# Layer-1 stacks with a gap behind each pair, and two heads of a pair in one 32-column tile

## Chip, cores and metric

The kernel runs on one core of a Trainium2 chip. The metric is the device time of one execution in microseconds (us). The core has a matrix engine (TensorE: PE for the matmuls, PEld for the weight loads), VectorE (DVE), ScalarE (ACT), GpSimd (POOL) and a queue engine (SyncE, SP) that issues nearly all DMAs. Data live in SBUF (128 partitions), matmul results in PSUM (eight banks of 128 x 512 f32), and intermediate tensors in DRAM.

## Reference

Two decoder layers on x (32 batch rows, 128 positions, 128 channels), each a post-norm chain of three blocks: layer 0 has a recurrent mix, a block of two attentions with an FC part, and an expert layer; layer 1 has a rotary self-attention, a cross-attention with silu in place of softmax, and an expert layer with capacities. The edit touches the first two blocks of layer 1:

```python
q = split_heads(x @ Wq + bq)          # 16 heads of 8
k = split_heads(x @ Wk + bk)
v = split_heads(x @ Wv + bv)
q, k = _rope(q), _rope(k)
scores = einsum('bhqd,bhkd->bhqk', q, k) / sqrt(8)
probs = softmax(scores)
out = einsum('bhqk,bhkd->bhqd', probs, v) ...  @ Wo + bo
# cross-attention: scores as above from x and ctx, masked, then
attn = silu(scores); out = einsum('bhqk,bhkd->bhqd', attn, v) ... @ Wo.T
```

## The kernel before

The 32 batch rows are worked on in eight groups of four (G = 4, GT = 512 tokens). Each block of a layer is a stage that yields, for each group, eight units with lags; the list `items` holds every step at its place and `pipeline` emits the steps in that order. The framework's scheduler then plans the order on each engine's queue from estimated durations and gives out the buffers of each pool (`w8`: seven slabs of 2,064 f32 columns; `PT`: two PSUM banks; `PV`: one, called the bank). Stages overlap: the self-attention (stage 5) starts under the expert layer of layer 0 (stage 4), and the cross-attention (stage 6) starts under the end of stage 5.

**Stacks.** Scores of layer 1 are computed from three bf16 parts of the f32 queries and keys. Heads have 8 channels, so the parts of one head are stacked into 48 rows. `spill` (L829 to L832) writes the parts of a group to a DRAM tensor `d_st` whose rows are [2 pars][8 pairs][query and key][512 tokens], and `stack` (L843) reads back, for one half of the heads and one parity, 48 or 50 rows of four pairs each: 8 KB in one piece per row. `scratch` (L816) fills the rows from 48 on from a constant. A group has four such reads: `take` issues two (one per parity) for each of the two halves.

**One self-attention step** j (0 to 7 in a group) is one half of the heads, h = j // 4, and one batch row, b = j % 4. `smax` computes the scores without the maximum (48 rows) and takes row maxima on DVE (L1000). `mrow`, `mwrite` and `mread` turn the maxima into two more rows of the stack by way of DRAM (`d_m`, L1013 and L1019). `probs` computes the scores again with these rows (50 rows) and exponentiates two banks on ACT (L1027). `values9` multiplies by V: V is kept per batch row as a tile of 16 x 9 columns (8 channels and a one for the sum of each head), and eight matmuls take 24 columns each, so that each head fills a block of 32 PSUM rows, four heads beside each other and two parities one after the other in columns. A copy on ACT (L875) brings 256 columns of the bank to `ob`. After both halves of a batch row, `norm` turns `ob` with four transposes (L1038), takes the reciprocal of the sums (L1041) and multiplies (L1044); `oproj` turns the result (L1056) and multiplies by Wo (L1062).

**V tiles.** `pad9` and `more9` cut V tiles out of `w8` slabs and preset them: POOL writes the ones and zeros (L858). `v9proj` adds the bias into them (L925); there are 20 for eight groups, used in turn. In the cross-attention, `valuesx` already lets two heads add into one 32-column block (L1194 is its copy of 128 columns); its V tiles (`vx`, L906) are slabs of `w8` too, and so are the expert weights of layer 1 (`cap_w13`, L1252).

`block` emits a list of matmuls that stay together (L169). All score and value matmuls of layer 1 have this line.

Of the kernel before, what the change touches and what calls it, by code (L numbers as in the profile page):

```python
# [9 lines left out]
F32 = mybir.dt.float32  # L10
FR = mybir.dt.float32r
BF = mybir.dt.bfloat16
U8 = mybir.dt.uint8
I32 = mybir.dt.int32
AF = mybir.ActivationFunctionType
ALU = mybir.AluOpType
# [3 lines left out]

G = 4
GT = G * 128

# [3 lines left out]
W8 = 7  # L29
VX = 10  # L30
V9 = 5
WV = 24
VT = 15 * 9 + WV

BUFS = dict(big=5, v=8, qk=3, e=6, pt=4, xs=4, cs=5, xb=2, msk=2, res=2, x=4)
TAG = dict(y="x", rres="res", wstage="xs", sx="xs", sc="cs", mask0="msk", v="v", qk="qk", e="e", p="pt",
           o="big", wo="big", sot="x", sxb="xb", sres="res", ctx="res", fx="xs", fxb="v", fh="big", fres="res", x1="x", fres2="res", lt="res",
# [35 lines left out]
class Net:  # L73
    def __init__(self, ctx, tc, a, ngroups):
# [15 lines left out]
        nc.gpsimd.tensor_copy(self.identb, self.ident)  # L90
        self.mhalf = self.cst.tile([128, G], F32, name="mhalf")
        nc.gpsimd.memset(self.mhalf, -0.5)
# [14 lines left out]
    def tok(self, tag):  # L107
        return self.t(tag, [G, 128])

# [93 lines left out]
    def half_turns(self, pts, es):  # L203

        calls = []
        for h in range(2):
            for b in range(G):
                for z in range(2):
                    r = slice(z * 64, z * 64 + 64)
                    calls.append((pts[z][:, (h * G + b) * 64:(h * G + b) * 64 + 64], es[h][r, b * 128:(b + 1) * 128],  # L210
                                  self.ident[r, r], None))
# [8 lines left out]
    def putx(self, g, x, final=False, queue=None):  # L220
        if final:
            d = self.a["out"][g * G:(g + 1) * G].rearrange("b s d -> s b d")
        else:
# [586 lines left out]
    def scratch(self, k):  # L810

        if self.dst is None:
            self.dst = []
            for i in range(3):
                d = self.dp.tile([64, 2, 8, 2, GT], BF, name=f"d_st{i}")
                self.nc.sync.dma_start(out=d[48:64], in_=self.a["pad_bf"])  # L816
                self.dst.append(d)
        return self.dst[k % 3]

# [4 lines left out]
    def spill(self, k, p):  # L824

        dma = self.nc.sync.dma_start
        d = self.scratch(k)
        rows = lambda lo, n: d[lo * 8:(lo + n) * 8].rearrange("(a d) r q z t -> (d r q) a z t", d=8)
        dma(out=rows(0, 3), in_=p)  # L829
        for z in range(2):  # L830
            dma(out=rows(3, 2)[:, :, z, :], in_=p[:, z:z + 2, z, :])
        dma(out=rows(5, 1)[:, 0], in_=p.rearrange("p a z t -> p (a z) t")[:, 0:6:5, :])  # L832
        return d

    def stack(self, d, h, n, slab=False):

        if slab:
            s = self.wp.tile([128, 4128], BF, name="w8", tag="w8", bufs=W8)
            s = s[:, 0:8 * GT].rearrange("p (q z t) -> p q z t", q=4, z=2)
        else:  # L840
            s = self.t("stack", [4, 2, GT], BF)
        for par in range(2):
            self.nc.sync.dma_start(out=s[par * 64:par * 64 + n], in_=d[0:n, par, h * 4:h * 4 + 4])  # L843
        return s

    def pad9(self):

        self.v9 = []
        t = self.w8()
        self.more9(t[:, 768:2064])  # L850
        return t[:, 0:768]

    def more9(self, t):
        for k in range(min(t.shape[1] // VT, V9 * G - len(self.v9))):
            c = t[:, k * VT:k * VT + VT]
            v = c[:, 0:144].rearrange("p (h c) -> p h c", c=9)
            self.nc.gpsimd.memset(v[:, :, 8:9], 1.0)
            self.nc.gpsimd.memset(c[:, 144:VT], 0.0)  # L858
            self.v9.append((v, c))

    def values9(self, j, v, ps, ob, last, scale=1.0):

        nc = self.nc
        pq, at = j // 4, j % 2
        o = self.bank()
        calls = []
        for par in range(2):
            c = (at * 2 + par) * 128
            for k in range(4):
                h = 2 * (pq * 4 + k) + par  # L870
                calls.append((o[k * 32:k * 32 + WV, c:c + 128], v[:, h * 9:h * 9 + WV], ps[par][:, k * 128:(k + 1) * 128],
                              dict(start=True, stop=True, tile_position=(0, k * 32))))
        self.block(calls, last)
        ob = ob or self.t("ob")
        nc.scalar.activation(ob[:, pq * 256:pq * 256 + 256], o[:, at * 256:at * 256 + 256], AF.Copy, scale=scale)  # L875
        return ob

    def bank(self):
# [36 lines left out]
    def v9proj(self, g, b, kh, kl, wh, wl, bv):  # L915

        vp = self.pst("v9")
        t = slice(b * 128, (b + 1) * 128)
        self.mm3(vp[:, 0:128], kh[:, t], kl[:, t], wh, wl)
        k = (g + 1) % V9 * G + b  # L920
        if k >= len(self.v9):
            self.more9(self.w8())
        v, c = self.v9[k]
        h8 = lambda t: t.rearrange("p (h d) -> p h d", d=8)
        self.nc.vector.tensor_tensor(v[:, :, 0:8], h8(vp[:, 0:128]), h8(bv), ALU.add)  # L925
        return c

    def att_w(self):
# [10 lines left out]
    def att_units(self, g, getw, done):  # L939
        nc, sm = self.nc, self.sm  # L940
        w = Later(getw)
        st = {}
# [91 lines left out]
        def norm(b):  # L1034
            ob = st.pop(("ob", b))
            tp = self.pst("norm")
            for s in range(4):
                nc.tensor.transpose(tp[:, s * 128:(s + 1) * 128], ob[:, s * 128:(s + 1) * 128], self.ident)  # L1038
            tv = tp.rearrange("p (h c) -> p h c", c=32)
            r = sm.tile([128, 16], F32, name="ar")  # L1040
            nc.vector.reciprocal(r, tv[:, :, 8])  # L1041
            if b == 0:
                st["ok"] = self.t("ok", [G, 16, 8])
            nc.vector.tensor_tensor(st["ok"][:, b], tv[:, :, 0:8], r.unsqueeze(2).to_broadcast([128, 16, 8]), ALU.mult)  # L1044

        def again():
            st["x"] = self.getx(g)
# [5 lines left out]
        def oproj():  # L1053
            tp = self.pst("oT")
            for b in range(G):
                nc.tensor.transpose(tp[:, b * 128:(b + 1) * 128], st["ok"][:, b].rearrange("p h d -> p (h d)"),  # L1056
                                    self.ident)
            oT = self.t("oT")
            nc.scalar.copy(oT, tp)
            o = self.pst("aout").rearrange("p (b d) -> p b d", d=128)  # L1060
            for b in range(G):
                nc.tensor.matmul(out=o[:, b, :], lhsT=oT[:, b * 128:(b + 1) * 128], rhs=w["wo"],  # L1062
                                 start=True, stop=True)
            res = st.pop("res")
            nc.vector.tensor_tensor(res, o, res, ALU.add)
            st["ln"] = self.ln(res, 1e-5, act=True)

        units = []
        for j in range(8):
            h = j // 4  # L1070
# [17 lines left out]
            if j == 7:  # L1088
                o = L6["oproj"]
# [475 lines left out]
def prep(i):  # L1565
    c = np.ascontiguousarray
    f = np.float32
    pairs = lambda w: c(w.reshape(8, 128, 128).transpose(1, 0, 2).reshape(128, 1024))
    d = {
        "xtok": c(i["x"].transpose(1, 0, 2)),  # L1570
        "xT": c(i["x"].transpose(2, 0, 1).reshape(128, 4096)),
        "ctxT": c(i["ctx_1024"].transpose(2, 0, 1).reshape(128, 4096)),
        "mask0": c(i["mask_BxS2_bk0"].reshape(4096)),
        "rwkv_w": c(np.concatenate([i["L0_attn_" + n].T for n in ("Wk", "Wv", "Wr", "Wo")], axis=1)),
        "rwkv_v": c(np.stack([i["L0_attn_" + n] for n in
                              ("mix_k", "mix_v", "mix_r", "spatial_decay", "spatial_first")], axis=1)),
    }
# [23 lines left out]
    b = [i["L1_attn_bq"], i["L1_attn_bk"]]  # L1601
    d["a1_b"] = c(np.stack([b[0][order], b[0][partner], b[1][order], b[1][partner]], axis=1))
    d["a1_bv"] = c(i["L1_attn_bv"])
    d["a1_bo"] = c(i["L1_attn_bo"])
    heads = np.array([2 * (pq * 4 + k) + par for pq in range(2) for par in range(2) for k in range(4)])
    rows = (heads[:, None] * 8 + np.arange(8)).reshape(128)
    d["a1_wo"] = c(i["L1_attn_Wo"][rows])
    inv = (np.float32(1.0) / np.power(np.float32(10000.0), np.arange(0, 8, 2, dtype=f) / np.float32(8))).astype(f)
    ang = np.arange(128, dtype=f)[None, :] * inv[order % 4][:, None]
    d["a1_cos"] = c(np.cos(ang).astype(f))  # L1610
# [8 lines left out]
    heads = np.array([8 * pq + 2 * k + par for k in range(4) for pq in range(2) for par in range(2)])  # L1619
# [28 lines left out]
```

## Time and profile before

| | |
|---|---|
| Median of 3 runs | 1808.09 us (1808.03 to 1809.1) |
| Profiled execution: time, span | 1817.27 us, 1815.5 us |
| Granted TensorE clock, mean | 0.961 |
| PE, PEld, DVE, ACT, POOL busy | 90%, 72%, 76%, 67%, 54% |
| DMA | 163.43 MB, mean 90 GB/s |
| Expert layer of layer 0 (L760), last step | 1217 us |
| Self-attention's exponentials (L1027) | 1217 to 1411 us |
| Cross-attention's copies (L1194) | 1390 to 1568 us |

All times of stages count from the span's start. A row of an instruction group names line, engine and operation, what is written from what, the shape and the number of instructions; then the busy time in us and the mean of one in ns; then the idle time of the engine before them, and what ended it. Durations of matmuls overlap, so their sum is more than PE's time. The chain of waits is followed back from the end of the span, at each step to what released it. Tiles have the names of the pools: `v` or `ob` are one pool, `e` are the exponentials, `big` the stacks, `qk` the parts, `S`, `mm`, `PT`, `PV` are PSUM.

### The profile page before, as it was taken

The numbers are of one execution on the slowest core, as the hardware profiler recorded it, in microseconds if no ns is written. First come the engines' busy times: TensorE is split into PE (matmuls) and PEld (weight loads), VectorE is DVE, ScalarE is ACT, GpSimd is POOL, SyncE is SP. The second block draws the span as 40 slices with busy tenths as digits, with TensorE's granted clock in tenths as the row PEclk, the third lists the DMA queues.
The fourth block names the chain that finished last, engine by engine and source line by source line (L and its number), as shares of the span: only waits on it lengthen the run. The fifth ranks groups of instructions, "written<-read, shape, count | busy, mean of one in ns | idle before, by whom it ended". The sixth has DMA issues, their size and how long they took to land.

```text
span 1815.5 us, 45617 instructions
## 1 busy us (share of the span) xinstructions
PE 1628.6 (90%) x15858; PEld 1311.8 (72%) x15858; DVE 1380.2 (76%) x5303; ACT 1214.1 (67%) x3889; POOL 982.6 (54%) x1324
## 2 busy tenths in 40 slices
PE   4898898899999999998899999998877887989898
PEld 2676676777777777776688888876655554778898
DVE  7879888887777777775676667778864775788896
ACT  3786777878888888887744554336666666656654
POOL 4657676777665555564534444345533443446455
PEclk7899999999999999999999999999989998899999
DMA  6100110111110000000123443336667987223222
GB/s 172 36 26 23 41 44 24 33 48 56 49 39 9 27 25 26 27 25 14 58 79 124 167 154 109 108 124 196 182 184 173 246 231 204 93 71 105 82 94 70
DMA packets 86214, 163.43 MB, mean 90 GB/s; under 512 B 12968, under 2 KB 34352, under 8 KB 80368
## 3 DMA queue, kind: packets, MB, share of 16 engines
q1 hardware_dynamic: 83248, 146.89, 27.5%
q0 software_dynamic: 1584, 11.54, 1.5%
q8 instruction: 125, 2.05, 0.5%
q10 hardware_dynamic: 1152, 2.10, 0.3%
q14 instruction: 105, 0.86, 0.2%
HBM read 106.75 MB, written 55.31 MB: 89 GB/s over the span
## 4 chain that ended last, share of the span: by engine, by line
PE 41%; DVE 20%; ACT 15%; POOL 11%; issue 6%; DMA 6%; SPq 1%; POOLq 0%; ACTq 0%; DVEq 0%
ACT e L483 8%; PE mm L157 5%; PE S L771 5%; PE PV L169 4%; PE mm L158 4%; PE mm L159 4%; DVE e L478 4%; PE S L169 3%; POOL x L255 3%; PE mm L541 3%; PE PT L1395 3%; POOL e L487 2%; DMA x<-x 2%; DVE x L263 2%; PE S L620 1%
## 5 line engine op out<-in xcount | busy, mean ns | idle before, releaser
L483 ACT ACTIVATE e<-e,nm 128x128 f32<-128x128 f32 x1024 | 398.8, 394 | 111.8 <-POOL nm L480 111.8
L487 POOL TENSOR_TENSOR e<-e,ri 128x512 f32<-128x512 f32 x256 | 268.4, 1054 | 175.2 <-DVE ri L485 146.2
L478 DVE CUSTOM_DVE_ANT_0 e<-S,msk 128x128 f32<-128x128 f32 x1024 | 227.9, 284 | 12.0 <-PE PT L168 9.1
L483 ACT ACTIVATION_READ_ACCUMULATOR e<-e,nm 128x1 f32 x1024 | 196.2, 192 | 0.0
L169 PEld LDWEIGHTS S<-qk 64*128 64x128 f32 x2048 | 128.3, 190 | 78.0 <-issue 40.6
L169 PE MATMUL S<-qk 64*128 64x128 f32 x2048 | 151.3, 287 | 30.2 <-DVE pt L501 16.3
L169 PE MATMUL PV<-pt,v 128*64 128x128 f32 x2048 | 141.9, 281 | 10.8 <-DVE big L523 10.6
L157 PE MATMUL mm<-xs,w 128*128 128x512 f32 x296 | 130.9, 446 | 16.5 <-ACT xs L150 5.0
L276 POOL TENSOR_SCALAR rsqv<-bmv 128x4 f32<-128x4 f32 (+1 forms) x73 | 22.5, 308 | 215.3 <-DVE bmv L243 179.9
L771 PEld LDWEIGHTS S<-w,v 128*128 128x128 f32 x1024 | 129.1, 191 | 10.2 <-ACT v L760 1.9
L760 ACT ACTIVATE v<-mm,col_moe_b 128x512 f32<-128x512 f32 x128 | 85.6, 686 | 75.4 <-PE mm L159 74.8
L771 PE MATMUL S<-w,v 128*128 128x128 f32 x1024 | 133.9, 276 | 1.7 <-ACT v L760 1.7
L485 DVE RECIPROCAL ri<-su 128x4 f32<-128x4 f32 x256 | 43.6, 172 | 120.7 <-ACT e L483 90.7
L169 PEld LDWEIGHTS PV<-pt,v 128*64 128x64 f32 x2048 | 110.9, 138 | 21.6 <-issue 6.7
L158 PE MATMUL mm<-xs,w 128*128 128x512 f32 x296 | 119.8, 405 | 1.6 <-DVE xs L151 1.4
L159 PE MATMUL mm<-xs,w 128*128 128x512 f32 x296 | 119.1, 402 | 0.0
L169 PE MATMUL PV<-e,w 128*32 128x128 f32 (+1 forms) x2048 | 90.3, 299 | 26.3 <-ACT e L1027 13.9
L501 DVE COPY pt<-PT 128x256 f32<-128x256 f32 x256 | 97.3, 415 | 8.4 <-ACT pt L501 7.6
L523 DVE TENSOR_TENSOR big<-PV,big 128x512 fp32r<-128x512 f32 x128 | 87.3, 682 | 19.5 <-ACT big L522 19.0
L1000 DVE TENSOR_REDUCE amx<-mm 128x4 f32<-128x512 f32 x128 | 82.1, 684 | 24.3 <-PE mm L169 24.2
L501 ACT COPY pt<-PT 128x256 f32<-128x256 f32 x256 | 81.8, 373 | 25.2 <-PE PT L168 25.0
L541 PE MATMUL mm<-big 128*128 128x512 f32 x384 | 96.9, 398 | 0.0
(326 smaller groups left out, 4803.7 us busy)
## 6 DMA issues: line engine op xcount, KB each, us to landing
x<-x SPq DMA_DIRECT2D x151, 256.0 KB
pt<-d_w SPq DMA_DIRECT2D x64, 256.0 KB
big<-d_st SPq DMA_DIRECT2D x32, 400.0 KB
d_st<-qk SPq DMA_DIRECT2D x48, 256.0 KB
d_st<-qk SPq DMA_DIRECT2D x16, 768.0 KB
big<-d_st SPq DMA_DIRECT2D x32, 384.0 KB
d_w<-big POOLq DMA_DIRECT2D x11, 1024.0 KB, 6.4
w<-d_w SPq DMA_DIRECT2D x7, 1024.0 KB
```

Of the source, the lines that this page charges most:

```text
L157: mm(out=out, lhsT=wh, rhs=xh, start=True, stop=False)
L158: mm(out=out, lhsT=wh, rhs=xl, start=False, stop=False)
L159: mm(out=out, lhsT=wl, rhs=xh, start=False, stop=True)
L169: return self.nc.tensor.matmul(out=out, lhsT=lhsT, rhs=rhs, **more)
L478: self.seen = nc.vector.tensor_tensor_reduce(e[:, t], s[h][:, t], msk[:, t], 1.0, NEG, ALU.add, ALU.max, mx[:, b:b + 1])
L483: nc.scalar.activation(e[:, t], e[:, t], AF.Exp, bias=nm[:, b:b + 1], scale=0.125, accum_out=su[:, b:b + 1])
L487: i = nc.gpsimd.tensor_tensor(e3, e3, ri.unsqueeze(2).to_broadcast([128, G, 128]), ALU.mult)
L501: last = (nc.vector.tensor_copy if h else nc.scalar.copy)(d, s_)
L523: nc.vector.tensor_tensor(lo, o, hi.bitcast(F32), ALU.subtract)
L541: nc.tensor.matmul(out=out, lhsT=a_, rhs=b_, start=n == 0, stop=n == 3 * PER - 1)
L760: nc.scalar.activation(h, hp, AF.Gelu, bias=w["b1"][:, k:k + 1])
L771: nc.tensor.matmul(out=o[:, b, :], lhsT=hs[i][:, b * 128:(b + 1) * 128], rhs=w["w2"][:, k * 128:k * 128 + 128], start=i == 0, stop=i == 1)
```

## The change

In DRAM, a row of a stack holds for each pair 1,024 elements and now 8 unused ones (16 bytes), so that the four pairs that one read takes are no longer adjacent; all writes and reads of `d_st`, in stage 5 and 6, follow. In the self-attention a V tile is now 8 x 27 columns: per pair, the even head's 9, nine zeros, the odd head's 9. The matmul of a head takes 18 columns (its own 9 and the zeros), and the two heads of a pair add into the same 18 rows of a block. The copy takes 128 columns in place of 256, `norm` has two transposes in place of four, and Wo is no longer reordered.

```diff
+GAP = 8
-WV = 24
-VT = 15 * 9 + WV
+VT = 8 * 27
...
-                d = self.dp.tile([64, 2, 8, 2, GT], BF, name=f"d_st{i}")
-                self.nc.sync.dma_start(out=d[48:64], in_=self.a["pad_bf"])
+                d = self.dp.tile([64, 2, 8, 2 * GT + GAP], BF, name=f"d_st{i}")
+                self.nc.sync.dma_start(out=d[48:64, :, :, 0:2 * GT], in_=self.a["pad_bf"].rearrange("p r q z t -> p r q (z t)"))
...
-        rows = lambda lo, n: d[lo * 8:(lo + n) * 8].rearrange("(a d) r q z t -> (d r q) a z t", d=8)
-        dma(out=rows(0, 3), in_=p)
+        rows = lambda lo, n: d[lo * 8:(lo + n) * 8].rearrange("(a d) r q x -> (d r q) a x", d=8)
+        dma(out=rows(0, 3)[:, :, 0:2 * GT], in_=p.rearrange("p a z t -> p a (z t)"))
         for z in range(2):
-            dma(out=rows(3, 2)[:, :, z, :], in_=p[:, z:z + 2, z, :])
-        dma(out=rows(5, 1)[:, 0], in_=p.rearrange("p a z t -> p (a z) t")[:, 0:6:5, :])
+            dma(out=rows(3, 2)[:, :, z * GT:(z + 1) * GT], in_=p[:, z:z + 2, z, :])
+        dma(out=rows(5, 1)[:, 0, 0:2 * GT].rearrange("p (z t) -> p z t", z=2), in_=p.rearrange("p a z t -> p (a z) t")[:, 0:6:5, :])
...
-            self.nc.sync.dma_start(out=s[par * 64:par * 64 + n], in_=d[0:n, par, h * 4:h * 4 + 4])
+            self.nc.sync.dma_start(out=s[par * 64:par * 64 + n].rearrange("p q z t -> p q (z t)"),
+                                   in_=d[0:n, par, h * 4:h * 4 + 4, 0:2 * GT])
...
-            v = c[:, 0:144].rearrange("p (h c) -> p h c", c=9)
-            self.nc.gpsimd.memset(v[:, :, 8:9], 1.0)
-            self.nc.gpsimd.memset(c[:, 144:VT], 0.0)
+            v = c.rearrange("p (q r c) -> p q r c", r=3, c=9)
+            self.nc.gpsimd.memset(v[:, :, 1, :], 0.0)
+            v = v[:, :, 0:3:2, :]
+            self.nc.gpsimd.memset(v[:, :, :, 8:9], 1.0)
...
-        pq, at = j // 4, j % 2
-        o = self.bank()
+        pq = j // 4
+        o = self.bank()[:, j % 2 * 128:j % 2 * 128 + 128]
...
-            c = (at * 2 + par) * 128
             for k in range(4):
-                h = 2 * (pq * 4 + k) + par
-                calls.append((o[k * 32:k * 32 + WV, c:c + 128], v[:, h * 9:h * 9 + WV], ps[par][:, k * 128:(k + 1) * 128],
-                              dict(start=True, stop=True, tile_position=(0, k * 32))))
+                c = (pq * 4 + k) * 27 + par * 9
+                calls.append((o[k * 32:k * 32 + 18, :], v[:, c:c + 18], ps[par][:, k * 128:(k + 1) * 128],
+                              dict(start=par == 0, stop=par == 1, tile_position=(0, k * 32))))
...
-        nc.scalar.activation(ob[:, pq * 256:pq * 256 + 256], o[:, at * 256:at * 256 + 256], AF.Copy, scale=scale)
+        nc.scalar.copy(ob[:, pq * 128:pq * 128 + 128], o)
...
-            for s in range(4):
+            for s in range(2):
                 nc.tensor.transpose(tp[:, s * 128:(s + 1) * 128], ob[:, s * 128:(s + 1) * 128], self.ident)
-            tv = tp.rearrange("p (h c) -> p h c", c=32)
-            r = sm.tile([128, 16], F32, name="ar")
-            nc.vector.reciprocal(r, tv[:, :, 8])
+            tv = tp[:, 0:256].rearrange("p (q c) -> p q c", c=32)[:, :, 0:18].rearrange("p q (r c) -> p q r c", c=9)
+            r = sm.tile([128, 8, 2], F32, name="ar")
+            nc.vector.reciprocal(r, tv[:, :, :, 8])
```

`v9proj`, the product in `norm` and the turn in `oproj` index the same elements in the new layout; `a1_wo` loses its row order.

## Prediction

> **What bounds the kernel now.** I read the list of engines first, then the busy time by stretch, then the chain of waits through the layer-1 self-attention, then the instruction groups and the records of single DMA packets. A change of 0.2% (3.6 us) is about what a measurement of this kernel can tell from none.
>
> ```profile
> PE 1628.6 (90%) x15858; PEld 1311.8 (72%) x15858; DVE 1380.2 (76%) x5303; ACT 1214.1 (67%) x3889; POOL 982.6 (54%) x1324
> ```
>
> TensorE is busy 90% of the span, but that is an average over stages. The stretch that the edit works on is the self-attention's own, from the first exponentials (1217 us) to the last (1411 us): 64 steps of one head half and one batch row each. (The cross-attention's stacks get the gap too, but in its own stretch, 1425 to 1540, the list of waits has no engine waiting for a d_st load.) The busy time by stretch (length, then PE, PEld, DVE, ACT, POOL busy, the granted clock, DMA share, GB/s) shows two regimes:
>
> ```profile
> 1250.00:1275.00 25.00, 22.42 (x390) 16.41 (x388) 21.27 (x50) 17.34 (x40) 15.27 (x18) 1.00 0.57 171
> ...
> 1300.00:1325.00 25.00, 19.36 (x344) 14.06 (x344) 19.52 (x51) 15.10 (x37) 14.09 (x19) 1.00 0.62 184
> ...
> 1400.00:1425.00 25.00, 22.57 (x353) 14.84 (x343) 16.70 (x52) 18.27 (x39) 6.58 (x10) 1.00 0.90 224
> ```
>
> Up to about 1300 nothing is full: a group of four batch rows takes 20.8 us (its output projection at 1254.3, 1275.1, 1295.9), of which DVE is busy some 18. After 1300, PE and DVE fall back while DMA rises. The chain of waits (start, length, what) says why. In the steady part:
>
> ```profile
> 1258.54 0.64 PE PV L169 x16
> 1259.18 0.33 PE S L169 x8
> ...
> 1260.62 0.87 PE PT L1038 x8
> 1261.50 0.57 PE PV L169 x16
> 1262.06 0.33 PE S L169 x8
> ...
> 1264.38 0.68 PE PV L169 x16
> ...
> 1265.09 0.39 ACT v L875
> 1265.47 1.00 ACT e L1027 x2
> 1266.48 0.14 issue
> 1266.61 0.67 PE PV L169 x16
> ```
>
> One step is a ring of 2.23 us (1264.38 to 1266.61): values (PV), a copy on ACT, two exponentials, values again. In the later part the longest pieces are transfers:
>
> ```profile
> 1301.42 7.11 DMA d_m<-m
> ...
> 1320.19 7.86 DMA big<-d_st
> ...
> 1365.82 6.35 DMA d_m<-m
> 1372.78 4.59 DMA big<-d_st
> ...
> 1391.76 6.26 DMA big<-d_st
> ```
>
> The stacks (d_st) are 18.7 us of this chain, the small writes of row maxima (d_m) that queue behind stacks and spills 13.5 us.
>
> **Part 1: the transposes.** The edit halves them, 128 to 64. The groups by line give their price and that of the copies:
>
> ```profile
> L1038 PE MATMUL PT<-ident,v 128*128 128x128 f32 x128 | 22.2, 292 | 6.3 <-ACT v L875 5.1 <-DVE w L912 1.2
> L875 ACT ACTIVATE v<-PV 128x256 f32<-128x256 f32 x64 | 24.7, 386 | 47.1 <-PE PV L169 41.1 <-DMA big<-d_st 3.0 <-PE S L169 2.9
> L1194 ACT ACTIVATE v<-PV 128x128 f32<-128x128 f32 x32 | 8.9, 277 | 17.3 <-PE PV L169 16.8 <-PE S L169 0.4
> ```
>
> The 292 ns overlap: eight take 0.87 us on the chain, 109 ns each, so 64 x 109 = 7.0 us of PE time go. On the chain between 1215 and 1427 I find 11 pieces of L1038 with 6.6 us together; half is **3.3 us**. The rest lies while PE waits for exponentials anyway (0.52 us idle before the values at 1264.38). The lower bound is 0: in the two steady pieces of 0.87 us, ACT stands in four normalisations (L261, 1261.45 to 1263.10), which wait for POOL's bnm and not for PE.
>
> **Part 2: the copies.** A copy shrinks from 386 to 277 ns, the row of the cross-attention's copy of that shape. 64 x 109 ns = 7.0 us of ACT would be the upper bound. But the next exponential also waits for the scores (S) that PE computes right after the values. After a 256-column copy that had waited, it starts 0.295 to 0.367 us later; after the 128-column copy of the cross-attention the next activation starts 0.295 to 0.357 us later in most cases, no earlier. Only where ACT comes to the copy without idling and the scores are ready does the length decide: 0.264 us to the next start against 0.157, in 8 of the 64 copies. 8 x 0.107 = **0.9 us**.
>
> **Part 3: the values matmuls.** Their number, moving columns and order stay; 24 weight columns become 18 and the second head adds onto the first. The cross-attention already runs this form with 32 columns: mean 301 ns against 296, 16 in 0.64 us both. I take 0. The bank's columns 256 to 511 are now left to the cross-attention, whose values wait for L875 where the stages overlap (0.48 us at 1399.70, 0.36 at 1408.36): **0.8 us** at most, 0 if waits go by the whole bank; I take 0.8. DVE's reciprocal (251 ns), product (287) and bias add (276) keep their element counts: 0.
>
> **Part 4: the gap.** A row of a stack was 8 KB in one packet; now it is four of 2 KB. Alone, an 8 KB packet of the expert weights has a median of 309 ns, a 2 KB packet of 84 (they follow each other every 80), so four make 320 to 336, 4 to 9% more. But stack packets last longer: median 522 ns (mean 558) in 1225 to 1425 with 50 rows, 614 in 1425 to 1550 with 48 rows, twice 309. Four 384 KB loads issued from 1494.3 to 1495.6 land at 1498.9, 1501.1, 1503.3 and 1505.6: 2.2 us each, so the packets share something that is nearly full. Where 2 KB packets of other tensors run beside six or more 8 KB packets they last 131 to 135 ns in the first stretch and 163 to 168 in the second: four are 532 or 652, 5% below 558 or 6% above 614. I take **0**, between these, for they are the nearest rows; the ends are -29% (four times 99, the first stretch's mean over all 2 KB packets, against 558) and +27% (four times 195, the median of the crowded ones in the second stretch, against 614). "SBUF — State Buffer" (section on the DMA port swizzle) says that the lowest 64 partitions reach only 8 of the 16 ports, whatever the packets: by it the -29% isn't to be had and the sum below stands; by the 99 ns it would be 14.3 us. Rows now begin at multiples of 2,064 bytes: the nearest row is the 508-byte loads, half of which start 4 bytes off, median 27 ns as for 512 bytes, so 0. "DMA: Bandwidth & Descriptors" (How a descriptor splits into AXI transactions) speaks against it: a transfer off a 256-byte boundary also fetches the bytes before it, on average 120 per 2,048, an estimated 6% of 18.7 us, and by it the sum below would be 3.9 us. SP issues the loads in about 0.3 us; 128 to 256 packets cost it 0.4 to 0.6, and SP mostly waits. The three pad loads (48 packets of 32 KB, 1.2 to 3.1 us each, at 31 to 38 us) become 768 packets of 84 to 105 ns: 48 x 84 to 105 ns = 4 to 5 us on each of 16 engines, against 3 x 1.2 to 3.1; they're early, and nothing waits for them until 1130: 0.
>
> **Part 5: the w8 slabs.** A V tile grows from 159 to 216 columns, so 20 of them need three slabs (6 + 9 + 5), not two (8 + 12), out of seven. The second is now asked for by the third V tile of group 0 (its bias add at 1116.8), but its memsets run at 1131.6, when the FC stage gives its slab back: that add waits some 15 us and holds one of two PT banks. PE is busy 30.00 of 30 us there with expert work, and the tile is first read after 1217: 0, or up to 2 us if PE runs out of work. The third comes at 1198, when expert slab one is free (the add was at 1197.5), and pushes the cross-attention's two memsets (1.7 us of POOL each) and the expert loads one slab later; the first load of stage 7 moves from 1220 to about 1321, the use is after 1557: 0. Larger memsets: 20 x about 0.1 us on POOL, hidden.
>
> **Sum.** 3.3 + 0.9 + 0.8 + 0 = 5.0 us off the profiled execution (span 1815.5, time 1817.27). Its median of runs is 1808.09; I take the same 5.0 off that: **1803 us**. One term has no row: the order on each queue is planned anew from estimated durations, for both signs; group periods of 20.8 us that grow to 24 or more in the later groups say that a changed order is worth a few us, and I put 4 on either side.
>
> **The rivals.** (a) *The cover is complete*: the transposes on the chain only uncover ACT's normalisations or the next exponentials, as in the steady groups. Left are the 0.9 us of copies: **1807**. For it: ACT idles 41.1 us before L875 for PE, so shorter ACT work is mostly idle time moved. (b) *The packets are the gain*: four 2 KB packets cost 396 rather than 558 ns. The 32.2 us of d_st and d_m on the chain shrink by 29%, 9.3 us: 1808.1 - 5.0 - 9.3 = **1794**. Against it: the landings every 2.2 us; six 8 KB packets in a row at 309 ns would be 1.85, so there is 16% to win at most, unless the packets share less than it seems. (c) *The packets are the loss, and it ends slower*: 780 against 614 ns, 27% of the 32.2 us, +8.7 against -5.0: **1812**. It decides from 15.5% on, 5.0 of 32.2, that is when four packets take over 645 ns where one took 558. For it: the DMA share of 0.90 in 1400 to 1425, so there is no room. That the gap doesn't split the packets can hardly be, as the pieces are no longer adjacent.
>
> **How the numbers follow.** Forecast 0.36, of which 0.28 falls beyond the 0.2% and 0.08 within, since it is near that bound (1804.5); (b) 0.14; (a) 0.27, of which 0.23 within and 0.04 slower by a worse order; (c) 0.23. Faster 0.42, same 0.31, slower 0.27. The range: down to 1795, leaving out most of (b); up to 1814, (c) with 2 us for the slabs. The forecast's own range is 1799 to 1807.
>
> **What would show it.** L1038 x64 at about the same 109 ns apart; copies x64 at 277 ns with ACT's idle time before them grown, not shrunk; steps still near 2.2 us; stack packets of 2 KB at 130 to 165 ns; the DMA pieces on the chain within 10% of 32 us; first exponentials still near 1217. It is wrong if group periods before 1300 change by over 1 us, or if the stretch from 1300 to 1425 changes by over 5.

## The result: slower by 0.65%

The changed kernel takes 1821.47 us (median of 7 runs, 1817.68 to 1832.15), the kernel before on the same chip 1808.22 us (7 runs). The ratio is 1.0065 with a 95% interval of 1.0046 to 1.0084: some 12 us slower, where 5 us faster was forecast, and outside the range. Below, microseconds from a ratio are (ratio - 1) x 1,810.

The profiled execution of the change took 1819.92 us (span 1818.1). That is only 2.6 us more than the profiled execution of before, because the latter (1817.27) was one of the slow ones of its kernel; it lost its time in code that both share: its expert layer ended at 1217.5 us, that of the change at 1213.0. So stages are compared from the end of the expert layer: the last exponentials of the self-attention come 193.7 us after it before and 198.9 us after the change, the output projection of the cross-attention's seventh group after 314.3 and 324.5, the end after 598.0 and 605.1. About 5 us are lost in the self-attention and as much in the cross-attention, with single executions that differ by several us; the timed ratios decide.

**Engines** (first list of the page): the work went as the edit says.

```profile
PE 1621.3 (89%) x15794; PEld 1302.5 (72%) x15794; DVE 1377.0 (76%) x5303; ACT 1208.8 (66%) x3889; POOL 985.0 (54%) x1324
```

64 PE instructions are gone, PE is 7.3 us less busy and ACT 5.3.

**Busy time by stretch** (columns as before):

```profile
1250.00:1275.00 25.00, 21.63 (x353) 15.05 (x346) 19.89 (x53) 15.11 (x38) 13.01 (x16) 0.93 0.65 180
1275.00:1300.00 25.00, 18.08 (x235) 11.98 (x234) 13.47 (x32) 11.66 (x27) 11.27 (x14) 0.80 0.70 185
1300.00:1325.00 25.00, 20.46 (x373) 14.50 (x374) 21.64 (x61) 14.40 (x35) 14.10 (x18) 1.00 0.55 153
1400.00:1425.00 25.00, 22.46 (x310) 14.13 (x311) 15.46 (x45) 16.40 (x34) 4.95 (x7) 0.86 1.05 246
```

Before, the second of these stretches was:

```profile
1275.00:1300.00 25.00, 22.54 (x368) 16.65 (x364) 22.01 (x56) 16.64 (x38) 15.87 (x19) 1.00 0.57 171
```

The steady part before 1300 has a hole: from 1275 to 1300 PE issues 235 matmuls where it issued 368, at a clock of 0.80. The fourth group takes 28.9 us from its first exponentials to the next group's, where it took 20.8.

**The chain of waits** in that place, and its transfers later on:

```profile
1275.65 7.59 DMA d_m<-m
...
1283.98 0.27 SPq L843
1284.26 0.05 issue
1284.31 0.37 SPq L843
1284.68 0.04 issue
1284.72 8.04 DMA x<-x
1292.76 0.14 issue
1292.89 1.09 PE PT L231 x4
1293.98 0.99 PE PV L169 x16
...
1365.39 6.00 DMA big<-d_st
...
1393.46 5.89 DMA big<-d_st
```

SP issues two stack loads (L843) and only then the load of x for the next group; x lands 8.04 us later, and PE stands before its transposes (L231). In the profile of before the same load was issued just ahead of the two stack loads, at 1286.7, and landed in 2.72 us. In the cross-attention the chain waited for x in two pieces before:

```profile
1500.35 9.36 DMA x<-x
...
1530.85 2.57 DMA x<-x
```

Now it waits in four, of 31 us together:

```profile
1482.80 9.75 DMA x<-x
...
1504.94 8.84 DMA x<-x
...
1526.51 10.21 DMA x<-x
...
1536.80 2.54 DMA x<-x
```

**Groups** (out<-in, shapes, count | busy, mean ns | idle before, releaser):

```profile
L877 ACT COPY v<-PV 128x128 f32<-128x128 f32 x64 | 17.1, 267 | 44.3 <-PE PV L169 40.4 <-PE mm L169 3.8
L1040 PE MATMUL PT<-ident,v 128*128 128x128 f32 x64 | 14.4, 302 | 5.0 <-ACT v L877 3.4 <-DVE w L914 1.2 <-DVE pt L1046 0.2
```

Copies and transposes have the forecast prices (267 for 277 ns; 302 for 292). They were costed rightly and bought nothing that shows.

### The profile page after: what moved, and what is told of

Its sections match the earlier page's. It is cut to its first block, busy times and chain, and to the rows that moved or that the text cites. A ratio compares the mean times of both kernels' runs of the same rounds, so it can differ in the third digit from the quotient of the medians.

```text
span 1818.1 us, 45488 instructions
## 1 busy us (share of the span) xinstructions
PE 1621.3 (89%) x15794; PEld 1302.5 (72%) x15794; DVE 1377.0 (76%) x5303; ACT 1208.8 (66%) x3889; POOL 985.0 (54%) x1324
## 4 chain that ended last, share of the span: by engine, by line
PE 40%; DVE 19%; ACT 14%; POOL 12%; DMA 7%; issue 7%; SPq 1%; POOLq 0%; ACTq 0%; DVEq 0%
ACT e L483 8%; PE S L771 5%; PE mm L157 5%; PE PV L169 4%; DVE e L478 4%; PE mm L158 3%; PE mm L159 3%; PE S L169 3%; DMA x<-x 3%; POOL x L255 3%; PE mm L541 3%; PE PT L1397 3%; POOL e L487 2%; DVE x L263 2%; DMA wst<-in_m_w_dram 2%
## 5 line engine op out<-in xcount | busy, mean ns | idle before, releaser
L169 PEld LDWEIGHTS PV<-e,w 128*32 128x32 f32 (+1 forms) x2048 | 50.7, 109 | 66.5 <-ACT e L1029 24.8
```

Of the source, the lines that this page charges most:

```text
L169: return self.nc.tensor.matmul(out=out, lhsT=lhsT, rhs=rhs, **more)
```

## Experiments

All ratios are against the kernel before on the same chip. The planned order of an engine means the order of its instructions in the built kernel.

### Which part costs: gap, slab, shared tile

The two halves of the edit separate cleanly: the gap alone leaves the planned order of PE, ACT, DVE and POOL as it was, and in its trace SP issues its DMAs in the order of before.

Gap alone: the diff's lines in `scratch`, `spill` and `stack` with GAP = 8, nothing else.

> The kernel before with the gap alone: rows of 2,064 bytes behind each pair, stack loads in 2 KB packets; the order on PE, ACT, DVE and POOL is the same as before. Theory G (the packets cost the 13 us): +10 to +16 us, the loss in 1220 to 1540. Theory S (the shared tile and the order that comes with it cost them): within 3 us of before. Theory W (the third slab costs them): within 3 us of before. If G holds in part only, the DMA share of the stretch 1425 to 1475 is near 0.98 here as in the changed kernel, not 0.92.

**1.0049 (1.0029 to 1.0068), +8.9 us.** Theory G, most of the loss, though below its range. The DMA share of the two halves of 1425 to 1475 is 0.91 and 0.99: it was 0.91 and 0.94 before, and 0.99 and 0.98 in the change.

Slab alone:

```diff
-VT = 15 * 9 + WV
+VT = 216
-            self.nc.gpsimd.memset(c[:, 144:VT], 0.0)
+            self.nc.gpsimd.memset(c[:, 144:159], 0.0)
```

> The kernel before with V tiles of 216 columns instead of 159, of which the added ones stay unused: the w8 slabs go as in the changed kernel (a third one, one load of expert weights for the last stage later), the rest is as before; 29 of 7,291 entries of PE's list move. Theory W: +8 us or more, with the first stretch of the last stage or the expert layer longer. Theories G and S: within 3 us of before.

**1.0006 (0.9990 to 1.0023).** Theory W falls.

Shared tile alone: the change with `d_st`, `spill` and `stack` as before.

> The changed kernel without the gap: stacks in rows of 8 KB as before, the two heads of a pair in one tile of 32 columns, half the transposes, third slab. Theory G: this is the forecast's own part, -5 us (1,803) or, with the transposes hidden, -1. Theory S: +10 to +16 us, nearly all of the loss. Theory W: as the run with the slab alone.

**1.0021 (1.0002 to 1.0040), +3.8 us.** None of the theories: a loss where a gain was forecast, but not the whole. With the gap's it makes 0.70%, the measured 0.65% within the intervals.

### Why the gap costs

Aligned gap in the change:

```diff
-GAP = 8
+GAP = 128
```

> The changed kernel with a gap of 256 bytes instead of 16, so that every row of 2 KB begins on a multiple of 256 bytes; packets and order are the same as in the changed kernel. Theory G by misaligned rows: back by most of the loss, 1,805 to 1,811. Theory G by the number of packets: 1,819 to 1,823, as the changed kernel. Theories S and W: 1,819 to 1,823.

**1.0046 (1.0029 to 1.0063).** 1817.2 us lies between the ranges. The interval reaches 1815 to 1821, so it excludes that most of the loss is due to the boundary alone, and not the other range.

Gap in one stage only (one DRAM tile, a view with gaps and a packed one):

```diff
+        return self.view(self.dst[k % 3], 8, 8192) if k < self.ng else self.view(self.dst[k % 3], 0, 0)
+    def view(self, d, gap, lo):
+        n = 2 * GT + gap
+        return d[lo * (n == 2 * GT):lo * (n == 2 * GT) + 1024 * n].rearrange("(n r q x) -> n r q x", r=2, q=8, x=n)
```

> The kernel before with the gap in the stacks of the self-attention alone (loads of 50 rows); the cross-attention's stacks lie packed in the same DRAM tile and are read in 8 KB packets. The order on PE, ACT, DVE and POOL is that of before. The gap alone cost 8 to 9 us. Theory X (the loss is in the cross-attention's stretch, whose transfers were already near full): +0 to +3 us. Theory Y (in the self-attention's waits, as the prediction's third rival had it): +6 to +9 us. If both share it: +3 to +6.

> The other half: the gap in the stacks of the cross-attention alone (loads of 48 rows), the self-attention's packed. Theory X: +6 to +9 us. Theory Y: +0 to +3 us. The two runs should add up to the 8 to 9 us of the gap alone, unless one stage's loss hides the other's.

**Self-attention 1.0031 (1.0018 to 1.0044), +5.6 us; cross-attention 1.0017 (1.0004 to 1.0031), +3.1 us.** Both share it, and 5.6 + 3.1 = 8.7 is the gap's 8.9.

2 KB packets without a gap (the values and Wo follow the new order of the heads), and with an aligned gap:

```diff
-            self.nc.sync.dma_start(out=s[par * 64:par * 64 + n], in_=d[0:n, par, h * 4:h * 4 + 4])
+            self.nc.sync.dma_start(out=s[par * 64:par * 64 + n], in_=d[0:n, par, h:8:2])
```

> The kernel before without any gap, where each half of the heads takes every second pair of a row instead of four neighbours: the stack loads come in 2 KB packets that begin on multiples of 2,048 bytes, with rows and spills where they were before; the order is that of before. Theory P (the number of packets costs the time): +7 to +10 us, as the gap alone. Theory M (rows off the boundaries cost it): within 3 us of before.

> The kernel before with a gap of 256 bytes behind each pair: 2 KB packets on multiples of 256 bytes, pitch of a pair 2,304 bytes. Theory P: +7 to +10 us. Theory M: within 3 us of before. If it lies between, both count.

**Packets 1.0005 (0.9988 to 1.0022); aligned gap 1.0017 (1.0000 to 1.0033).** Theory P falls: four times as many packets cost nothing that can be measured. The aligned gap may cost something of its own: the 3.1 us here, and 3.4 us in the change (1817.2 with the aligned gap, 1813.8 for the shared tile alone, on one chip). By what, stays open: a spill that lands alone lands there in 2.13 to 2.15 us, sooner than before (below).

Packed stacks, 16 and 64 bytes off (8 and 32 elements):

```diff
-                d = self.dp.tile([64, 2, 8, 2, GT], BF, name=f"d_st{i}")
+                d = self.dp.tile([129, 8192], BF, name=f"d_st{i}").rearrange("a b -> (a b)")[8:1048584]
+                d = d.rearrange("(n r q z t) -> n r q z t", r=2, q=8, z=2, t=GT)
```

> The kernel before, whose stacks lie packed as before but begin 16 bytes off: all rows are off the 256-byte boundaries, stack loads still come in packets of 8 KB, spills are written in the pieces of before. Order as before on all engines. Theory R (what costs is the reading of 2 KB packets that begin off a boundary): within 3 us of before, as there are a quarter as many beginnings. Theory S (what costs is the writing of the spills off a boundary, which happens here as with the gap): +4 to +7 us, with writes of 1 KB at 50 to 51 ns and not 46 in the second half.

> As the run with the packed stacks 16 bytes off (+0.85%, some 15 us), but 64 bytes off: order, packets and pieces the same. Theory 64 (what matters is that a row begins and ends within a 64-byte line): within 3 us of before, 1 KB writes at 46 ns in the second half. Theory 256 (what matters is the 256-byte boundary): +10 to +16 us as with 16 bytes, 1 KB writes near 62 ns.

**16 bytes: 1.0085 (1.0066 to 1.0104), +15 us; 64 bytes: 1.0039 (1.0024 to 1.0053), +7 us.** No gap, 8 KB packets, the order of before, and more lost than by the whole change: theory S in kind, and twice its size. With 64 bytes half of it is left, so a 64-byte line is not boundary enough.

Reads off the boundary, writes on it (`spill` writes by `d` and hands the shifted view to the loads):

```diff
+                f = self.dp.tile([129, 8192], BF, name=f"d_st{i}").rearrange("a b -> (a b)")
+                d, self.late[i] = (f[o:o + 1048576].rearrange("(n r q z t) -> n r q z t", r=2, q=8, z=2, t=GT) for o in (0, 8))
```

> The kernel with stack loads in 2 KB packets on the boundary (+0.05%), whose stack loads now begin 16 bytes further on in memory than the rows that the spills write; the loads so bring each row shifted by 8 elements, and the attentions are computed from those. Writes stay on the boundary. Theory W (the writes pay): within 3 us of before. Theory R (the reads pay): +6 to +10 us, as the gap alone.

**1.0007 (0.9992 to 1.0021).** Theory W: the writes pay, not the reads. The traces show it at the place where nothing but the group's next spill is under way: the first spill of a group (L832 of before, 256 KB; the four shortest of each trace) lands in 2.42 to 2.50 us from its issue before and with reads off, in 2.71 to 2.87 with the gap alone, in 3.52 to 3.72 with 16 bytes. Under load, the spills issued from 1411 to 1531 us land after 5.7 to 5.9 us on average before, with 2 KB packets and with reads off; after 6.2 with the aligned gap and with 64 bytes, 7.1 with the gap alone, 7.3 in the change, 8.8 with 16 bytes. The mean 1 KB packet of that stretch lasts some 46 ns before, with 2 KB packets, with an aligned gap and with reads off; 50 with the gap and with 64 bytes; 62 with 16 bytes. In the queue's row of the stretch (packets, MB, share of the 16 engines), here of before, 2 KB packets, 16 bytes off, and the change, in this order, a megabyte fills more of the engines where the spills are off:

```profile
q1 hardware_dynamic: 12080, 27.79, 88.3%
```

```profile
q1 hardware_dynamic: 15240, 27.24, 86.9%
```

```profile
q1 hardware_dynamic: 11807, 26.79, 92.6%
```

```profile
q1 hardware_dynamic: 15340, 28.21, 94.2%
```

That is 3.18, 3.19, 3.46 and 3.34% for a MB. With 64 bytes it is 3.11 (27.70 MB, 86.1%): the 7 us of that run do not show in this measure.

### Why the shared tile costs

In its planned order two stack loads of a half stand ahead of loads of x on SP in three groups (at 1263, 1284 and 1309 us in the change). (From about 1320 us on, SP's order differs in further places, loads of x and of stacks against writes of row maxima above all; no run takes these apart.) The loads of x put ahead again, and the mirror image, the kernel before with SP's order of the change in just these three groups:

```diff
-                u += [(0, load), (L6["pre"], pre), (L6["spill"], spill)]
+                u += [(0, load, -99), (L6["pre"], pre), (L6["spill"], spill)]
-                u += [(L6["norm"] - 2, again), (L6["norm"], bias)]
+                u += [(L6["norm"] - 5, again), (L6["norm"], bias)]
```

> The shared tile without the gap, as in the run of that name (1,813.8, 0.21% above before), but with the loads of x (the next group's input and the residual) asked for a little earlier in the program, so that SP issues them before the two stack loads in three of the groups, as in the kernel before; PE, ACT and DVE keep the order of the shared tile's run. Theory Q (the new order on SP, which puts 800 KB of stacks ahead of x, took the gain): 1,803 to 1,808, so 5 to 9 us come back. Theory H (halved transposes and shorter copies are hidden, and something in the shared form itself costs 4 us): 1,812 to 1,816.

With the second argument true, `getx` is ordered behind the last two stack loads of a first half:

```diff
         def load():
-            st["x"] = self.getx(g)
+            st["x"] = self.getx(g, g == 7)
...
         def again():
-            st["x"] = self.getx(g)
+            st["x"] = self.getx(g, g in (2, 3, 4))
```

> The kernel before, with nothing else changed than that SP issues the two stack loads of a half before a load of x in three places of the self-attention, as it does in the changed kernel. Theory Q: +4 to +9 us, with loads of x that land after some 8 us, not 2.6 to 2.9, at 1281 and 1304, and PE's transposes of x waiting for them. Theory H: within 3 us of before.

**Loads of x ahead: 1.0009 (0.9994 to 1.0025), +1.6 us, 1811.4. The kernel before with stacks ahead: 1.0022 (1.0009 to 1.0036), +4.0 us.** The second shows theory Q: the order of these loads in three groups by itself costs what the shared tile costs. Its chain of waits has the pieces that were expected, of the loads of x issued behind stacks:

```profile
1284.81 8.38 DMA x<-x
...
1308.62 0.18 SPq L845
1308.80 0.05 issue
1308.85 0.33 SPq L845
1309.18 0.04 issue
1309.23 8.70 DMA x<-x
```

With the loads of x ahead, the only such piece of that stretch is 3.08 us long:

```profile
1302.66 3.08 DMA x<-x
```

The profiles bear the order out: the fourth group takes 27.0 to 28.9 us in the four kernels with stacks ahead (the change, the change with the aligned gap, the shared tile alone, the kernel before with stacks ahead) and 20.8 to 24.0 us in the other sixteen. The time of the first run lies between the ranges of Q and H, next to H's: its interval (-1.1 to +4.5 us) holds no loss as well as the whole of the shared tile's 3.8, and excludes the forecast gain of 5 us. So the transposes were put back:

```diff
-            for s in range(2):
-                nc.tensor.transpose(tp[:, s * 128:(s + 1) * 128], ob[:, s * 128:(s + 1) * 128], self.ident)
+            for s in range(4):
+                nc.tensor.transpose(tp[:, s * 128:(s + 1) * 128], ob[:, s % 2 * 128:(s % 2 + 1) * 128], self.ident)
```

> The kernel with the shared tile and the loads of x ahead, with four transposes a batch row again (two of them repeat the others), so 128 as before, and copies of 128 columns. The prediction's first part put the halved transposes at 3.3 us (0 to 7): by it this is 3.3 us slower than the kernel with the loads of x ahead. By its rival of the complete cover: within 1 us of that one.

**1.0010 (0.9991 to 1.0028),** against 1.0009 without: 64 transposes more on PE cost nothing that shows. The medians differ by 0.1 us; but the means of twelve runs each differ by 1.2, give or take 3.5, so that the 3.3 us are not excluded. In the profiles the pieces of these transposes on the chain go from 2.68 us (6 pieces) to 6.98 us (10), about as in the kernel before (6.6), and the copies' idle time from 43.7 to 48.2:

```profile
L1039 PE MATMUL PT<-ident,v 128*128 128x128 f32 x128 | 23.6, 309 | 3.5 <-ACT v L876 2.1 <-DVE w L913 1.4
```

### Transfers as the cover

A load of 50 rows raises its semaphore 11 times in the trace, one of 48 rows 16 times, one of 2 rows 3 times. "DMA: Bandwidth & Descriptors" (section on why a DMA increments its semaphore by 16) says that a DMA from this queue runs on the largest number of engines up to 16 that divides its slowest dimension on both sides (here the rows), and that what is left of 16 is added at once. That makes 10 updates for 50 rows and one more for the six added at once, which are the 11.

```diff
-            self.nc.sync.dma_start(out=s[par * 64:par * 64 + n], in_=d[0:n, par, h * 4:h * 4 + 4])
+            for lo, hi in ((0, 48), (48, 50))[:n - 47]:
+                self.nc.sync.dma_start(out=s[par * 64 + lo:par * 64 + hi], in_=d[lo:hi, par, h * 4:h * 4 + 4])
```

> The kernel before, whose self-attention stack loads of 50 rows are issued as 48 rows and 2 rows, one load more for each of the 32 (0.3 us each on SP); the order on the other engines is the same. Theory T (a load of 50 rows runs on ten of sixteen engines, which are full): the 48 rows land with 16 updates, and the self-attention gets 3 to 8 us shorter. Theory U (the engines are not the limit): within 3 us of before, or slower by SP's 32 more issues.

The other kernel takes `self.stack(st["d"], h, 64)`.

> The kernel before, whose self-attention stack loads take 64 rows and not 50 (14 more, which nothing reads): 28% more bytes, no more loads. Theory T: 16 updates a load, at most four packets of 8 KB on an engine where there were five, 2 to 5 us shorter. Theory U: 0 to +4 us by the added bytes.

**48 and 2 rows: 0.9983 (0.9971 to 0.9995), -3.1 us; 64 rows: 1.0007 (0.9992 to 1.0021).** The first is the lower end of theory T, and its interval (-0.9 to -5.2) reaches into theory U; the second is theory U. That the wider spread and the 28% more bytes cancel with 64 rows is one reading, which no run shows.

> The shared tile without the gap, loads of x ahead, stack loads of 48 and 2 rows. If the transfers were what covered the halved transposes and copies, they now show: 2 to 5 us below the split alone (1,807.3), 1,802 to 1,805. If the ring of exponentials, values and scores covers them: within 2 us of the split alone.

> The kernel before with stack loads of 48 and 2 rows, as measured before (0.9983, 0.9971 to 0.9995): 2 to 5 us below the kernel before.

**Split with the shared tile and loads of x ahead: 0.9961 (0.9945 to 0.9977), 1804.1 us; split alone, again: 0.9971 (0.9957 to 0.9986), 1806.05 us.** Both beat the kernel before (1810.81 there), by 7 and 5 us: the gain of the split is shown twice, the engines as its cause are not. The shared tile's part is 2 us, with intervals that overlap: it may begin to show once the transfers give way, and that is not shown.

## Why the prediction was wrong, by its steps

**Part 4, the gap at 0: the step that failed.** It priced the loads, which are read, by the lengths of their packets, and never priced the spills, which are written. Its row for rows off the boundary was the 508-byte loads, reads again, and reads off the boundary do cost nothing that shows (1.0007). Writes off it do: 15 us at 16 bytes, without any gap. The gap costs 8.9 us in all. Of these the aligned gap keeps some 3, from a cause that stays open; the rest fits the boundary, though the intervals of the two runs overlap (1.0029 to 1.0068 and 1.0000 to 1.0033).

For the packets its 0 held: 2 KB packets cost nothing that shows (1.0005). From 1205 to 1600 us that run has 25,152 packets of 2 KB with 3,162 us together; with the 14,208 of other tensors taken out at the 100.5 ns that they have before, 158 ns are left for one, 634 for four. One packet of the stacks before lasts 617 ns on average (2,022 us of 8 KB packets, less 335 for the 896 of the expert weights, over 2,736). These are estimates from the packets' records: 3% more, within the prediction's 5% less and 6% more.

The estimate from "DMA: Bandwidth & Descriptors" (bytes fetched before the start) is about reads and came to 1.1 us, which lies within the interval of the run with reads off: no run here shows or excludes it.

**Part 4, the cross-attention.** It was left aside because no engine waits there for `d_st`. It pays 3.1 us (0.7 to 5.6), with the DMA share already at 0.91 to 0.94 before. Through which wait is not shown: the chain of the change waits longer for x there, but with the aligned gap it waits for x for 55 us, and that run loses 3.1 us in all.

**"One term has no row": the planned order, 4 us on either side.** On the kernel before it came out at +4.0 us, the edge of what was allowed, and it need not have been left without a row: x landed in 2.7 to 3.0 us when issued ahead of two stack loads, and the second of two stack loads in 6.7 to 8.6, so what lands behind them comes some 5 us later; such swaps in three groups made 4.0 us.

**Parts 1 to 3 (5.0 us) and rival (a).** No gain showed: with the order put right the shared tile is at +1.6 us (-1.1 to +4.5), which excludes the 5.0. The transposes of **part 1** (3.3 us) seem hidden, as the rival had it: putting them back changed nothing that shows, though 3.3 us lie within the noise of that comparison. The step in doubt is that half of the time on the chain of waits was taken for time that can be won. **Part 2** (0.9 us) was not tested by itself; the idle time before the copies did not grow, as forecast, but fell (47.1 to 44.3). **Part 3** held for the value matmuls, 297 for 296 ns; its 0.8 us for the bank no run takes apart. **Part 5** held: 1.0006.

**Rivals (b) and (c).** Packets of 2 KB were neither a gain nor a loss. Rival (c) had the sign, and its +8.7 us for the gap stand beside the measured 8.9 by luck: its point was four packets over 645 ns where one took 558, and by the estimate above they took 634 where one took 617.

**What would show it:** copies x64 and transposes x64 were seen, and steps of 2.22 us (values at 1265.91 and 1268.13). The sign for being wrong, group periods before 1300 off by over 1 us, came true in the fourth group: 28.9 for 20.8.

## What to carry to other kernels

Price writes and reads of a layout apart: here a pad that moved the rows of a scratch off their boundary was paid by the writes, while reads off it cost nothing that shows. After an edit of the computing alone, still compare the order of the DMA queue with the old one: a big load that slips ahead of a small one that an engine waits for can cost up to the difference of their landings, here some 5 us a time. And look at a DMA's row count: splitting 50 rows into 48 and 2 was worth 3 to 5 us, where all the work that this edit saved did not show.

## What the runs showed of the hardware

With rows that all begin 16 bytes off, 25 MB of spills (48 writes of 256 KB and 16 of 768) cost 15 us more; with the gap's changing offset 9 us, of which an aligned gap keeps some 3; 64 bytes off 7 us. Why 64 bytes still cost is not settled: a lone spill lands there in 2.47 to 2.54 us, hardly later than before.

A DMA share well under one does not mean that transfers cost nothing: the self-attention's stretches have a share of 0.57 to 0.90 before, its loads of 50 rows post 11 updates and those of 48 rows 16, and splitting them gained 3 to 5 us.

A wait can cost more than its length. In the change's chain PE issues nothing from 1288.11 until x is there at 1292.89, 4.78 us; the busy time by stretch then has

```profile
1289.00:1293.00 4.00, 0.11 (x1) 0.14 (x2) 0.06 (x1) 0.00 (x0) 3.60 (x4) 0.79 0.89 194
1293.00:1297.00 4.00, 4.00 (x40) 2.49 (x40) 0.69 (x1) 2.25 (x5) 1.22 (x2) 0.50 0.20 42
```

a granted clock of 0.50 for the 4 us behind it: four transposes of x take 1.09 us and 16 value matmuls 0.99, in the group before 0.44 and 0.56 to 0.63. "TensorE: Matmul & The Clock Gate" (HAM oscillation) says that the matrix engine falls to half its clock when it idles for a window of some 3.4 us. This row agrees: the clock's records go to 0.50 at 1291.32, 3.2 us after the last matmul, and stay there for 6.83 us. But such an idle stretch isn't needed: in the same trace the clock is at 0.50 from 1257.18 to 1260.60, though PE was busy for 2.4 of the 3.4 us before. So a late transfer of 5 us can be paid again, in part, at half speed; between 1210 and 1420 us the records have 34 us at 0.50 in the change and 27 before.
